# A convolution, a Fourier layer and a gated recurrence on one core: pools exchanged at the hand-over into the recurrence, first columns stored first, part of a normalisation on GpSimd

## The chip, the cores and the metric

The kernel runs on one core of one Trainium2 chip. The metric is the device time of one execution in microseconds (us), as the median of several runs. Everything is float32. Besides these times there is one profiled execution, whose trace records each instruction with its engine (PE is TensorE, DVE VectorE, ACT ScalarE, POOL GpSimd, SP SyncE) and each DMA packet.

## The reference

The input `x` has 8 samples of 32 channels of 256 x 256. Four layers follow each other, each as a residual around a group normalisation `_gn` with 16 groups:

```
x = x + fourier(_gn(x))      # rfft2, 2 x 32 x 32 modes mixed over channels, irfft2, bias
x = x + conv5x5(_gn(x))      # one 5 x 5 kernel for every channel
x = x + recurrence(_gn(x))   # a gated cell from column to column, 256 columns
x = x + mix(_gn(x))          # running maxima in four directions, 1 x 1 convolution over 5 x 32
```

The cell of the recurrence takes the column before at three heights (96 inputs) and the column itself (32 inputs):

```
r = sigmoid(r_i + r_h);  z = sigmoid(z_i + z_h);  n = tanh(n_i + r * n_h)
new = n * z + cur * (1 - z)
```

where `_i` comes from the column before and `_h` from the current, normalised column. So each column needs the one before: the recurrence is a chain of 255 steps. Its group statistics need all of the convolution's output.

## The kernel before

Four functions follow each other, each with pools of on-chip memory of its own that are opened at its start and closed at its end.

`forward_and_mix` transforms `x`, and mixes the modes with the Fourier weights in eight steps (tile `xf` holds the spectrum, `wt` the weights, `sm` the results). The mixed spectrum goes to a buffer `smd` in device memory (L287).

`inverse_and_conv` works on 16 units (sample b, half of the channels) of two times eight channels. `load_spectrum` reads `smd` back (L350, L352), `spectrum` scales and corrects it (from L358), `load` reads `x` (L379, tile `xb`, on POOL's queue), `over_rows` and `over_columns` transform back with matmuls (L401, L418) and add x into one of five large column tiles `x1` (L427). `conv` runs the 5 x 5 convolution as matmuls (L487), and L520 scales the result and adds it to `x1` in place. Squares for the statistics run on ACT (L444, L527) and DVE. `statistics` and `keep` turn them into a mean and a scale for each group (from L556, with a power on POOL at L569), held in `stb` (L575). `store` writes each `x1` to `x2d` in device memory with 12 DMAs, three for each of four row groups a: L541 the middle columns, L545 the first 30, L546 the last 30. They are on SP's queue; for the very last `x1`, half are on ACT's queue. While the last unit is under way, POOL's queue loads the first eight columns of samples 0 to 6 into the tile `first` (L659).

`recurrence` then goes through 32 blocks of eight columns. Its 8 samples are two halves of four (x is 0 and 1), which take turns: while PE works for one half, the other engines finish the other. `load` reads a block of raw columns into `xw` (L724; for block zero only sample 7 is missing in `first`, L727). The statistics are transposed into `turned` (L707), `shift` follows (L711), and `normalise` writes xn = raw * scale + shift on ACT, 128 x 256 at a time, which is one sample and half a block of columns (L733). A block is normalised while the block before it is computed, one tile in each half step; block zero is normalised in one go before the first step. In a half step, `gates` issues PE's matmuls (L753, L761), including those of the next half step on the current column; then sigmoids on ACT (L828, L830, L831), `n` on DVE (L829, L834), tanh (L835), the product `a` of 1 - z and the current column on POOL (L837), two operations on DVE (L840, L842) that give the new column `hs`, and the sum with the raw column on POOL (L843). L840 is made to wait for `a`:

```
product = nc.gpsimd.tensor_tensor(a, zm, cur, ALU.mult)
...
ins = nc.vector.tensor_tensor(m, m, z, ALU.mult)
tc.add_manual_dep(ins.ins, product.ins.name, AFTER, reason="the sum behind it then need not wait")
```

DVE also keeps a running maximum `fm` (L864) and block statistics `bst` (L875).

`maxima_and_mix` reads the stored columns and maxima and computes the last layer.

Each engine runs its instructions in the order in which the program issues them. Pools are laid one after another in memory in the order in which they are opened. A tile that lies where a tile of a closed pool lay waits for what used it, and where it lies over a pool of tiles that live for the whole stage, it waits for all uses of that pool. In the inverse stage the pools are opened as

```
one = ctx.enter_context(tc.tile_pool(name="a2c", bufs=1))   # bias, junk, x1
xp = ctx.enter_context(tc.tile_pool(name="a2x", bufs=1))    # spectra, x
wk = ctx.enter_context(tc.tile_pool(name="a2w", bufs=2))    # tt
```

so `x1` lies low and x and spectra above it; in the recurrence `one` (`turned`, `shift2`, `hs`, `bst`) lies lowest, then `xn`, `xw` and `fm` in one pool, then the small tiles of a step (`rs`, `n`, `zm`, `a`, `zs`).

Of the kernel before, what the change touches and what calls it, by code (L numbers as in the profile page):

```python
# [16 lines left out]
P = 128  # L17
# [6 lines left out]
A = 4  # L24
# [272 lines left out]
def inverse_and_conv(tc, k, d, smd, xmean, x2d, stb, first):  # L297
# [13 lines left out]

    PLACES = (1, 2, 3, 5, 6, 7, 8)
    with ExitStack() as ctx:
        one = ctx.enter_context(tc.tile_pool(name="a2c", bufs=1))
        xp = ctx.enter_context(tc.tile_pool(name="a2x", bufs=1))
        wk = ctx.enter_context(tc.tile_pool(name="a2w", bufs=2))
        sm = ctx.enter_context(tc.tile_pool(name="a2s", bufs=3))
        ps = ctx.enter_context(tc.tile_pool(name="a2p", bufs=1, space=PSUM))

# [214 lines left out]
        def store(u, ch):  # L534
            b, h = units[u]
            c0 = 2 * CH * h + CH * ch
            x1, to = x1_of(u, ch), x2d[b, :, :, c0 : c0 + CH].rearrange("w a c q -> w a (c q)")
            for a in range(A):
                r = 32 * a
                queue = nc.scalar if a % 2 and 2 * u + ch == 2 * n - 1 else nc.sync  # L540
                queue.dma_start(  # L541
                    out=to[TS + 2 : TS * (NT - 1) + 2, a].rearrange("(t w) n -> w t n", w=TS),
                    in_=x1[r + 2 : r + 30, 2:NT].rearrange("w t c q -> w t (c q)"),
                )
                queue.dma_start(out=to[0 : TS + 2, a], in_=x1[r : r + 30, 1].rearrange("w c q -> w (c q)"))  # L545
                queue.dma_start(  # L546
                    out=to[TS * (NT - 1) + 2 : W, a], in_=x1[r + 2 : r + 32, 0].rearrange("w c q -> w (c q)")
                )

        def statistics(u):  # L550
            b, h = units[u]
# [20 lines left out]
        def keep(u, st):  # L572
            b, h = units[u]
            for kind in range(2):
                nc.vector.tensor_copy(  # L575
                    by_pair(stb[:, kind, b, 2 * CH * h : 2 * CH * (h + 1)]), twice(st[:, kind], 2)
                )
# [15 lines left out]
        with tc.manual_schedule(engines=None):  # L593
# [20 lines left out]
            for u in range(n):  # L614
# [44 lines left out]
                            nc.gpsimd.dma_start(out=first[:, b], in_=columns(x2d, b, 0, 8))  # L659
                if more:  # L660
                    squares(u + 1, 1, 1, 1, NT)
            keep(n - 1, statistics(n - 1))
            store(n - 1, 1)
            tc.declare_fence(nc.tensor.drain().ins, group="conv")
# [19 lines left out]
def recurrence(tc, k, d, x2d, x3d, fwd, stb, first, loaded, mean1, mv3):  # L684
# [9 lines left out]
    BC = B // NC  # L694
    with ExitStack() as ctx:
        one = ctx.enter_context(tc.tile_pool(name="bc", bufs=1))
        blk = ctx.enter_context(tc.tile_pool(name="bb", bufs=2))
        wk = ctx.enter_context(tc.tile_pool(name="bw", bufs=2))
        ps = ctx.enter_context(tc.tile_pool(name="bp", bufs=1, space=PSUM))
# [12 lines left out]

        hs = [[one.tile([P, BC, Q + 2], F32, name=f"hs_{x}_{i}") for i in range(NH)] for x in range(NC)]
        for t in hs[0] + hs[1]:
            nc.vector.memset(t, 0.0)
        bst = one.tile([P, B, NB, 6], F32, name="bst")

        raws, norms, psums = {}, {}, {}
# [1 line left out]
        def load(bi):  # L720
            if bi:
                t = blk.tile([P, B, WB, Q], F32, name=f"xw_{bi}", tag="xw", bufs=4)
                for b in range(B):
                    nc.sync.dma_start(out=t[:, b], in_=columns(x2d, b, bi * WB, (bi + 1) * WB))  # L724
            else:
                t = first
                nc.sync.dma_start(out=t[:, B - 1], in_=columns(x2d, B - 1, 0, 8))  # L727
            raws[bi] = t
            norms[bi] = blk.tile([P, B, WB, Q], F32, name=f"xn_{bi}", tag="xn")

        def normalise(bi, b, half):
            w = slice(half * WB // 2, (half + 1) * WB // 2)
            nc.scalar.activation(  # L733
                norms[bi][:, b, w], raws[bi][:, b, w], AF.Identity, bias=shift[:, b : b + 1], scale=sc[:, 1, b : b + 1]
            )
# [464 lines left out]
```

## Time and profile before

| quantity | value |
|---|---|
| median of 3 runs | 3066.25 us (3065.99 to 3067.99) |
| profiled execution, its own time | 3069.01 us |
| its span, first to last instruction | 3067.2 us |
| mean granted TensorE clock | 0.956 |
| busy: PE, DVE, ACT, POOL | 2796.5, 2585.2, 1870.4, 858.2 us |
| last statistic of the convolution written (L575 ends) | 1025.84 us |
| first sigmoid of the recurrence (L828) | 1046.03 us |
| last mixed spectrum stored (L287 issued) | 292.74 us |
| first spectrum back in use (L358) | 317.74 us |

Times in a trace count from the first instruction. A row of the timeline gives start, duration, engine, source line, operation, tile written and tiles read, and in brackets the engine's idle time before it with the instruction or DMA that ended it. SPq and ACTq are a queue's DMA issues, whose duration is the time to issue, not to transfer.

### The profile page before, as it was taken

To read this page: it belongs to the slowest core of one execution; us is meant where nothing else is said; L and a number is where in the kernel's file an instruction comes from. 1 tells how busy PE (TensorE), PEld (TensorE's weight loads), DVE (VectorE), ACT (ScalarE), POOL (GpSimd) and SP (SyncE) were. 2 spreads that over 40 slices of the span, in tenths; PEclk is the share of its full clock that TensorE was granted. 3 is DMA by queue.
4 is the path that set the end of the run, shared out by engine and by line. 5 is a ranking of instruction groups with operands and counts; after the bars stand their busy time and mean duration, and the time that the engine had idled before them with its cause. 6 is when DMAs were issued, how large, how long until landed. Compare 5 with 4: busy or idle time off the path is not lost.

```text
span 3067.2 us, 111686 instructions
## 1 busy us (share of the span) xinstructions
PE 2796.5 (91%) x47736; PEld 1645.3 (54%) x47736; DVE 2585.2 (84%) x5178; ACT 1870.4 (61%) x4482; POOL 858.2 (28%) x1247
## 2 busy tenths in 40 slices
PE   7986799999999799999999999999999588888887
PEld 4665344444444466666666666666666233333333
DVE  5752587778888589999999999999999799999997
ACT  3432377676777578888888888888887222222222
POOL 0110011111111355555555555555555200000000
PEclk9985899999999899999999999999999799999998
DMA  9977577777775565667666676666764588888885
GB/s 385 392 283 222 154 230 225 218 224 219 231 221 165 146 148 139 142 158 167 148 142 141 154 167 151 144 142 149 167 157 115 180 327 329 328 330 329 330 327 226
DMA packets 468193, 655.69 MB, mean 214 GB/s; under 512 B 328784, under 2 KB 329696, under 8 KB 441456
## 3 DMA queue, kind: packets, MB, share of 16 engines
q1 hardware_dynamic: 407528, 487.89, 54.6%
q0 software_dynamic: 16784, 84.11, 8.4%
q10 hardware_dynamic: 43384, 76.55, 6.9%
q8 instruction: 374, 6.13, 0.8%
q14 instruction: 123, 1.01, 0.1%
HBM read 371.63 MB, written 272.63 MB: 210 GB/s over the span
## 4 chain that ended last, share of the span: by engine, by line
PE 69%; DVE 20%; DMA 5%; issue 3%; ACT 2%; SPq 0%; ACTq 0%; POOL 0%; DVEq 0%; POOLq 0%
PE r L753 14%; PE z L753 13%; PE vp L487 11%; PE ni L753 6%; PE nh L753 6%; PE up L418 4%; DVE rv L1012 4%; PE yp L131 3%; DMA spec<-smd 3%; DVE dq L1018 2%; DVE uq L1020 2%; DVE m L1026 2%; DVE m L1024 2%; DVE m L1022 2%; PE sp L158 2%
## 5 line engine op out<-in xcount | busy, mean ns | idle before, releaser
L761 PE MATMUL z<-hs,weights 64*64 64x256 f32 x4080 | 539.2, 382 | 0.0
L761 PE MATMUL ni<-hs,weights 64*64 64x256 f32 x4080 | 525.7, 375 | 0.0
L761 PE MATMUL r<-hs,weights 64*64 64x256 f32 x4080 | 525.0, 375 | 0.0
L843 POOL TENSOR_TENSOR xw<-xw,hs 128x256 f32<-128x256 f32 x496 | 340.2, 686 | 635.3 <-DVE hs L842 635.3
L1058 ACT ACTIVATE ot<-o,bres 128x512 f32<-128x512 f32 x256 | 155.1, 688 | 505.1 <-PE o L1043 489.7
L487 PE MATMUL vp<-x,c_conv 64*64 64x384 f32 (+5 forms) x4608 | 428.8, 491 | 4.9 <-DVE x L520 4.9
L520 DVE SCALAR_TENSOR_TENSOR x<-vp,r,x 128x128 f32<-128x128 f32 (+2 forms) x640 | 350.6, 563 | 87.9 <-PE vp L487 75.1
L837 POOL TENSOR_TENSOR a<-zm,xn 128x256 f32<-128x256 f32 x510 | 373.1, 732 | 7.0 <-ACT zm L830 6.7
L835 ACT ACTIVATE n<-n,bih 128x256 f32<-128x256 f32 x510 | 259.5, 509 | 186.4 <-DVE n L834 186.4
L1043 PE MATMUL o<-m,wsc 32*32 32x512 f32 x3072 | 228.8, 724 | 108.0 <-DVE m L1026 104.4
L753 PE MATMUL r<-hs,weights 64*64 64x256 f32 x2040 | 318.9, 389 | 4.4 <-DVE hs L842 3.4
L753 PE MATMUL z<-xn,weights 64*64 64x256 f32 x2040 | 305.8, 377 | 14.9 <-DMA xw<-x2d 14.9
L487 PEld LDWEIGHTS vp<-x,c_conv 64*64 64x64 f32 x4608 | 222.4, 132 | 180.0 <-issue 104.4
L753 PE MATMUL r<-xn,weights 64*64 64x256 f32 x2040 | 305.3, 376 | 2.1 <-ACT rs L828 2.1
L753 PE MATMUL nh<-xn,weights 64*64 64x256 f32 x2040 | 306.2, 377 | 0.0
L753 PE MATMUL z<-hs,weights 64*64 64x256 f32 x2040 | 305.3, 376 | 0.0
L753 PE MATMUL ni<-hs,weights 64*64 64x256 f32 x2040 | 305.1, 375 | 0.0
L733 ACT ACTIVATE xn<-xw,shift,turned 128x256 f32<-128x256 f32 x496 | 290.3, 586 | 0.0
L829 DVE SCALAR_TENSOR_TENSOR n<-nh,bhh,rs 128x256 f32<-128x256 f32 x510 | 246.2, 483 | 46.4 <-ACT rs L828 32.6
L761 PEld LDWEIGHTS ni<-hs,weights 64*64 64x64 f32 x4080 | 284.8, 133 | 0.3
L761 PEld LDWEIGHTS r<-hs,weights 64*64 64x64 f32 x4080 | 280.9, 131 | 0.2
L828 ACT ACTIVATE rs<-r,brz 128x256 f32<-128x256 f32 x510 | 241.7, 474 | 54.2 <-PE r L761 33.8
(162 smaller groups left out, 6230.3 us busy)
## 6 DMA issues: line engine op xcount, KB each, us to landing
xb<-in_xl_dram POOLq DMA_DIRECT2D x96, 768.0 KB, 7.6
xa<-in_xt_dram SPq DMA_DIRECT2D x64, 1024.0 KB
x<-x3d SPq DMA_DIRECT2D x32, 2048.0 KB
fw<-fwd SPq DMA_DIRECT2D x32, 2048.0 KB
out_dram<-ot ACTq DMA_DIRECT2D x64, 1024.0 KB
xw<-x2d SPq DMA_DIRECT2D x248, 256.0 KB
fwd<-fm SPq DMA_DIRECT2D x248, 256.0 KB
x3d<-xw SPq DMA_DIRECT2D x248, 256.0 KB
```

The costliest lines, as they stand in the source:

```text
L487: ins = nc.tensor.matmul(vps[bank][to, :, dst], lhsT=k.conv[r, P : P + 64] if kind == 2 else k.conv[r, o], rhs=pair_of(u, ch, g, lo, hi, s ...
L520: nc.vector.scalar_tensor_tensor(x, src[o], r1[rows, g : g + 1], x, ALU.mult, ALU.add, accum_out=s1[rows, 0, n, ch, g : g + 1])
L733: nc.scalar.activation(norms[bi][:, b, w], raws[bi][:, b, w], AF.Identity, bias=shift[:, b : b + 1], scale=sc[:, 1, b : b + 1])
L753: ins = nc.tensor.matmul(out[r], lhsT=weights[r, kind, gate, :], rhs=src[r], start=start, stop=stop)
L761: ins = nc.tensor.matmul(out[pairs[1 - i]], lhsT=weights[r, kind, gate, :], rhs=prev[r, :, q0 : q0 + Q], start=False, stop=stop,)
L828: rs = nc.scalar.activation(r, p["r"], AF.Sigmoid, bias=brz[:, 0:1])
L829: nc.vector.scalar_tensor_tensor(m, p["nh"], bhh[:, 2:3], r, ALU.add, ALU.mult)
L835: nc.scalar.activation(m, m, AF.Tanh, bias=bih[:, 2:3])
L837: product = nc.gpsimd.tensor_tensor(a, zm, cur, ALU.mult)
L843: nc.gpsimd.tensor_tensor(raw, raw, new, ALU.add)
L1043: nc.tensor.matmul(pts[b2][i][32 * j : 32 * j + 32].rearrange("p (w q) -> p w q", q=Q), lhsT=wsc[q, b2, t, :], rhs=src[j][q, b2], start=first,
L1058: nc.scalar.activation(ot[:, i], pts[b2][i], AF.Identity, bias=bres[:, b2, i : i + 1])
```

## The change

It has five parts. In `inverse_and_conv` the pool of `x1` is opened after those of x, spectra and `tt`, so that x and spectra lie low and `x1` above; in `recurrence`, `xn` gets a pool of its own, opened next to `one`, so that the lowest tiles and `xn` lie over spectra and x, and `xw`, `fm` and a step's small tiles over `tt` and `x1`. The stores of each `x1` write the first columns before the middle ones, and the last store writes the first columns of all four row groups, then all middle ones, then all last ones, on SP's queue alone. A sigmoid of one column is put ahead of the last statistics, with which the table is loaded there. The memsets of `hs` cover only the two border columns. The load of sample 7 into `first` is issued on POOL. And block zero's second half is normalised by GpSimd: samples 0 to 3 ahead of the first step, samples 4 to 7 in columns 1 and 2; GpSimd also normalises samples 0 to 3 of the first half of block one, in columns 4 and 5, and ACT starts with block one in column 2.

```
     with ExitStack() as ctx:
-        one = ctx.enter_context(tc.tile_pool(name="a2c", bufs=1))
         xp = ctx.enter_context(tc.tile_pool(name="a2x", bufs=1))
         wk = ctx.enter_context(tc.tile_pool(name="a2w", bufs=2))
+        one = ctx.enter_context(tc.tile_pool(name="a2c", bufs=1))
...
-            for a in range(A):
-                r = 32 * a
-                queue = nc.scalar if a % 2 and 2 * u + ch == 2 * n - 1 else nc.sync
...
+            last = 2 * u + ch == 2 * n - 1
+            parts = [(a, part) for a in range(A) for part in range(3)]
+            for a, part in sorted(parts, key=lambda x: x[1]) if last else parts:
+                r, queue = 32 * a, nc.sync
+                if part == 0:
+                    queue.dma_start(out=to[0 : TS + 2, a], in_=x1[r : r + 30, 1].rearrange("w c q -> w (c q)"))
+                elif part == 1:
...
+            nc.scalar.activation(junk[:, 0, 0:1], k.mhalf[:, 0:1], AF.Sigmoid)
             keep(n - 1, statistics(n - 1))
             store(n - 1, 1)
...
+        xnp = ctx.enter_context(tc.tile_pool(name="bn", bufs=2))
         blk = ctx.enter_context(tc.tile_pool(name="bb", bufs=2))
...
         for t in hs[0] + hs[1]:
-            nc.vector.memset(t, 0.0)
+            nc.vector.memset(t[:, :, 0 : Q + 2 : Q + 1], 0.0)
...
-                nc.sync.dma_start(out=t[:, B - 1], in_=columns(x2d, B - 1, 0, 8))
+                nc.gpsimd.dma_start(out=t[:, B - 1], in_=columns(x2d, B - 1, 0, 8))
             raws[bi] = t
-            norms[bi] = blk.tile([P, B, WB, Q], F32, name=f"xn_{bi}", tag="xn")
-
-        def normalise(bi, b, half):
+            norms[bi] = xnp.tile([P, B, WB, Q], F32, name=f"xn_{bi}", tag="xn")
+
+        def normalise(bi, b, half, other=False):
             w = slice(half * WB // 2, (half + 1) * WB // 2)
+            if other:
+                nc.gpsimd.tensor_scalar(
+                    norms[bi][:, b, w], raws[bi][:, b, w], sc[:, 1, b : b + 1], shift[:, b : b + 1], ALU.mult, ALU.add
+                )
+                return
...
-            for half in range(2):
-                for b in range(B):
-                    normalise(0, b, half)
+            for b in range(B):
+                normalise(0, b, 0)
+            for b in range(BC):
+                normalise(0, b, 1, True)
             for bi in range(NB):
                 for wi in range(WB):
                     if wi == WB // 2 and bi + 2 < NB:
                         load(bi + 2)
                     for x in range(NC):
                         step(bi * WB + wi, x)
-                        if bi + 1 < NB:
+                        if bi == 0 and 1 <= wi < 3:
+                            normalise(0, BC + NC * (wi - 1) + x, 1, True)
+                        if bi == 0 and 4 <= wi < 6:
+                            normalise(1, NC * (wi - 4) + x, 0, True)
+                        if bi + 1 < NB and (bi or wi > 1):
                             half, b = divmod(NC * wi + x, B)
                             normalise(bi + 1, b, half)
                     running(bi, wi)
```

More of the change, by code (lines that the diff above doesn't have):

```diff
@@ L537, in store @@
             x1, to = x1_of(u, ch), x2d[b, :, :, c0 : c0 + CH].rearrange("w a c q -> w a (c q)")
-            for a in range(A):
-                r = 32 * a
-                queue = nc.scalar if a % 2 and 2 * u + ch == 2 * n - 1 else nc.sync
[L541 to L548, printed above, removed]
+            last = 2 * u + ch == 2 * n - 1
[5 more added lines that the diff above has]
+                elif part == 1:
+                    queue.dma_start(
+                        out=to[TS + 2 : TS * (NT - 1) + 2, a].rearrange("(t w) n -> w t n", w=TS),
+                        in_=x1[r + 2 : r + 30, 2:NT].rearrange("w t c q -> w t (c q)"),
+                    )
+                else:
+                    queue.dma_start(
+                        out=to[TS * (NT - 1) + 2 : W, a], in_=x1[r + 2 : r + 32, 0].rearrange("w c q -> w (c q)")
+                    )
         def statistics(u):
@@ L726, in load @@
                 t = first
-                nc.sync.dma_start(out=t[:, B - 1], in_=columns(x2d, B - 1, 0, 8))
+                nc.gpsimd.dma_start(out=t[:, B - 1], in_=columns(x2d, B - 1, 0, 8))
             raws[bi] = t
-            norms[bi] = blk.tile([P, B, WB, Q], F32, name=f"xn_{bi}", tag="xn")
-        def normalise(bi, b, half):
+            norms[bi] = xnp.tile([P, B, WB, Q], F32, name=f"xn_{bi}", tag="xn")
+        def normalise(bi, b, half, other=False):
             w = slice(half * WB // 2, (half + 1) * WB // 2)
+            if other:
+                nc.gpsimd.tensor_scalar(
+                    norms[bi][:, b, w], raws[bi][:, b, w], sc[:, 1, b : b + 1], shift[:, b : b + 1], ALU.mult, ALU.add
+                )
+                return
             nc.scalar.activation(
```

## The prediction

> **What bounds the kernel now.** I read the page first: PE is busy 91% of the 3067.2 us and the chain of waits lies on PE.
>
> ```profile
> PE 69%; DVE 20%; DMA 5%; issue 3%; ACT 2%; SPq 0%; ACTq 0%; POOL 0%; DVEq 0%; POOLq 0%
> ```
>
> No matmul is removed, so what can be won lies where PE stands still. The slices and the timeline show two hand-overs. The large one is from convolution to recurrence; the timeline shows it (start, duration, engine, line; the bracket is idle time before and who ended it):
>
> ```profile
> 1021.29 0.95 ACT L527 ACTIVATE junk<-x 128x896 f32<-128x896 f32 x1 [1.81 <-DVE x L520]
> ...
> 1025.66 0.18 DVE L575 COPY stb<-st 128x16 f32<-128x16 f32 x1 [1.76 <-POOL st L569]
> ...
> 1034.23 0.98 DVE L707 STREAM_TRANSPOSE turned<-stb 128x768 f32<-128x768 f32 x1 [8.40 <-DMA x2d<-x]
> ...
> 1035.43 0.16 DVE L711 SCALAR_TENSOR_TENSOR shift<-turned 128x8 f32<-128x8 f32 x1
> ...
> 1035.76 7.98 ACT L733 ACTIVATE xn<-first,shift,turned 128x256 f32<-128x256 f32 x16 [13.43 <-DVE shift L711]
> 1037.88 1.12 PE L753 MATMUL z<-xn,weights 64*64 64x256 f32 x4 [14.88 <-DMA xw<-x2d]
> ...
> 1044.73 1.28 ACT L828 ACT_TABLE_LOAD   x1
> 1046.03 0.47 ACT L828 ACTIVATE rs<-r,brz 128x256 f32<-128x256 f32 x1
> ```
>
> The reader is to see three waits: the transpose of the statistics is ready at 1025.84 but waits 8.40 us for the last stores to land, because `turned` lies where the convolution's columns lay; then ACT normalises 16 + 2 tiles; then it loads a table. PE's last matmul for r ends near 1042.75, 3.3 us before the sigmoid that reads it.
>
> The small hand-over is from mixing to the inverse transform, the same view:
>
> ```profile
> 292.74 0.36 SPq L287 DMA_DIRECT2D smd<-sm  x1
> 296.54 0.52 SPq L350 DMA_DIRECT2D spec<-smd  x1
> 297.50 3.16 POOL L379 DMA_DIRECT2D xb<-in_xl_dram  x6 [83.64 <-issue]
> 317.74 0.69 DVE L358 TENSOR_SCALAR spec<-spec 64x1024 f32<-64x1024 f32 x1 [25.02 <-DMA spec<-smd]
> ```
>
> Here x is loaded (4.7 MB) only after the mixed spectrum is stored, and shares the DMA engines with the spectrum's load, which the chain waits for.
>
> Last, one half step of the recurrence in block zero:
>
> ```profile
> 1060.48 0.43 PE L753 MATMUL r<-hs,weights 64*64 64x256 f32 x2
> 1060.51 0.69 POOL L843 TENSOR_TENSOR first<-first,hs 128x256 f32<-128x256 f32 x1 [1.43 <-DVE hs L842]
> 1061.15 0.73 POOL L837 TENSOR_TENSOR a<-zm,xn 128x256 f32<-128x256 f32 x1
> 1061.38 0.51 ACT L835 ACTIVATE n<-n,bih 128x256 f32<-128x256 f32 x1 [0.36 <-DVE n L834]
> 1062.00 0.43 DVE L840 TENSOR_TENSOR n<-n,zs 128x256 f32<-128x256 f32 x1 [0.65 <-ACT n L835]
> ```
>
> The product `a` starts only when POOL's addition ends; it ends at 1061.88, 0.12 us before L840, which is made to wait for it. In the other half steps `a` ends 0.47 us before. POOL has almost no room here.
>
> **What the Trainium skill says.** "ScalarE: Activation LUTs", What ACT_TABLE_LOAD costs: about 1283 ns for a switch of sets; the trace agrees (1.28). "GPSIMD Engine Reference", 3.1 Elementwise: 2.6 cycles an element with two inputs, 1.03 to 1.8 with one, at 1.2 GHz. For 256 columns that is an estimate of 0.55 us with two; the trace has 0.69 and 0.73, so some 0.15 is fixed. "DMA: Bandwidth & Descriptors", Queues, rings and completion order: each DMA engine takes its queues in turn, packet by packet. The trace agrees: from 302 to 311 us it holds about 70 packets of 6 KB a microsecond from POOL's queue and about as many of 128 bytes from SP's. "SBUF — State Buffer", Who interferes with whom: a VectorE instruction with two SBUF inputs contends with a GpSimd one that reads SBUF. The trace fits: L864 takes from 0.67 to 1.16 us for one shape.
>
> **The change, part by part.**
>
> *Pools exchanged, and xn in its own.* In the inverse stage x, spectra and tt now lie lowest, the columns `x1` above. In the recurrence `turned`, `shift2`, `hs`, `bst` lie over spectra and x, `xn` over x, all long free. So the transpose needs only L575: 1025.9 to 1026.9, shift at 1027.1 (its 0.16 follows the transpose as before). That is 1035.6 - 1027.1 = 8.5 us. The eight full memsets (2.25 us of DVE) become strided ones of two columns, issued in the last unit but one; at some 0.07 each (as the smallest DVE rows) I charge 0.3 in all.
>
> *The wait that takes its place.* `rs`, `n`, `zm`, `a` and `xw` still lie over the columns, so the first sigmoid, first product and SP's block-one loads wait for all twelve last stores. Those now go on SP alone (ACT loses six issues). They are bound by transfer, not by issue: 2.1 MB took 1022 to 1033.3, 186 KB/us; the twelve before, on SP alone, took 969.8 to 982. Now the four first-column pieces can start at 1018.9, since they need only the first two tiles (L520 ends 1018.8), and 1.85 MB remains from 1022.2: 10 us, plus 0.7 for the load of `first`, plus 0.8 to land gives 1033.7.
>
> *Eighth `first` load on POOL.* It now waits for the first-column pieces only (landed near 1022.5), stands behind the power L569 (to 1025.63), takes 0.89 to issue, and 3.9 to 5 us to land: about 1030.5. Behind it on POOL are four normalisations, then the two additions; none is needed before `a` near 1035.4. ACT normalises sample seven at 1031; PE wants it about 6.1 us after shift, 1033.2.
>
> *ACT.* Eight normalisations (0.5 us apart) instead of 18 ahead of the sigmoid; the table load moves to 1022, where ACT is idle, a dummy sigmoid with it. So the sigmoid follows PE: before, r was complete 7.2 us after shift, so 1034.3; with the stores at 1033.7 plus or minus 1, I take 1034.6. Gain 1046.0 - 1034.6 = **11.4 us**, of which 8.5 is the wait and the rest the 10 activations and the table.
>
> *POOL inside the steps.* Eight normalisations are put into half steps of columns 1, 2, 4, 5, after the addition and ahead of the next `a`. Queued behind each are `a` and, through it, L840, L842 and PE's next gates. The kernel before has no such instruction on POOL. Bounds for T: 0.35 (one input at 1.03 cycles plus 0.15) and 1.0 (half as long again as the 0.69 row); I take 0.5, from 1.8 cycles. Four fall where `a` has 0.2 us of room with PE's own, four where it has 0.4: 4(T - 0.2) + 4(T - 0.4) = 8T - 2.4 = **1.6**, with port contention 1.8; at the ends 0.4 and 5.6.
>
> *Mixing to inverse.* `xb` now lies over `xf` and waits for the last mixing matmul (290.97) instead of the stores: it starts 6.4 us sooner, ahead of the last two stores, whose 128 packets per DMA engine now alternate with its 48 large ones. By work: POOL's data from 292.6, 12.1 us of DMA, 2.6 for the stores, landed at 307 to 308; spectrum issued 0.4 later (the bias load now stands before it), 5.5 us of data, landed near 316 to 318 against 317.6. Bounds: -4 (stores get through first) to +2; I take **-1.0**.
>
> Middle pieces second instead of first in the other 31 stores: the same bytes on the same queue, nothing waits for one piece; 0. PE's order is unchanged. After its pause PE's clock is low for a while in the trace (matmul pairs 0.43 us apart instead of 0.21 from 1047.3 to 1050.5, costing 0.9); I let it stay as it is.
>
> Sum: -11.4 + 1.8 - 1.0 + 0.3 = **-10.3 us**. The profiled execution has span 3067.2 and took 3069.0, 2.8 over the median 3066.25; its sum would give 3058.7, on the median 3056.0.
>
> **The rivals.** *Re-bound hand-over*: stores on SP at the pace of the contended set (12 in 14.8 us), or `first` landing 7 us after issue, set the sigmoid near 1038, and T is 1.0: -8 + 5.6 - 1.0 + 0.3, about -3 to -7, 3061. For it: the sigmoid really waits for all stores, with 0.6 us to spare. Against: no other loads run then.
>
> *More than forecast*: stores pass x quickly and T is 0.35: -11.4 + 0.4 - 4 + 0.3, 3051.5. The packet counts speak against.
>
> *GpSimd becomes the bound (slower)*: if one normalisation with per-partition scalars takes T, the gain of 12.1 is used up at T = 1.8, and from 1.8 the four ahead of the additions delay the first `a` too. It is slower by 0.2% from 2.3 us; at 2.5, 8 x 2.5 - 2.4 + 4 x 0.7 = 20.4, or +8, 3074. For it: the power takes 1.66 us for 8 columns, so POOL can be slow. Against: its plain operations keep to the estimate.
>
> *It does not do what it says*: `turned` could wait for the stores after all; the addresses in the built program exclude that, and xn's too.
>
> **How the numbers follow.** 0.2% is 6.1 us, about what a measurement of this kernel can tell from no change. Forecast 0.62; re-bound 0.22, of which 0.14 still over 0.2%; more 0.08; GpSimd 0.08, of which 0.07 over. Faster 0.84, same 0.09, slower 0.07. The range runs from more than forecast to just past re-bound: 3050.5 to 3062.5.
>
> **What would show it.** Right: the transpose near 1026 with no DMA as releaser, the table load near 1022, first sigmoid 1034 to 1036, block zero's half steps in columns 1, 2, 4, 5 longer by 0.1 to 0.6 us, the spectrum's scaling at 314 to 318. Wrong: the sigmoid released by a store after 1037; POOL's xn over 1 us; the spectrum after 320.

## The result and the profile after

The changed kernel takes 3055.6 us (median of five runs, 3052.2 to 3058.3); the kernel before, measured beside it, 3068.0. The ratio is 0.9955, with a 95% interval of 0.9942 to 0.9967: faster by some 12.4 us. The forecast was 3056.0, so the total is right, but partly by luck, for its parts are not: the trace shows one gain of 9.5 us that the prediction put at nothing, and GpSimd's instructions inside the steps cost 4.3 us where 1.8 were forecast.

First the line of the page with the shares of the chain of waits, after:

```profile
PE 65%; DVE 20%; issue 3%; DMA 2%; ACT 1%; POOL 1%; SPq 0%; DVEq 0%; ACTq 0%; POOLq 0%
```

DMA has fallen from 5% to 2%, and POOL, which had 0%, is on the chain now. Three per cent of the span would be 90 us, far more than was won: a chain can pass through the one or the other of two things that end together. Such shares tell where to look, not how much; the stages tell that.

The profiled executions, cut at four instructions that both have (first scaling of a spectrum L358; last copy of the statistics, L575 before and L579 after; first and last sigmoid of r, L828 and L839). Each time is the distance between starts in the timeline, in us:

| stage | before | after | difference | forecast |
|---|---|---|---|---|
| start to first L358 | 317.7 | 319.4 | +1.6 | -1.0 |
| inverse transform and convolution, to the last statistics | 707.9 | 698.4 | **-9.5** | 0 |
| hand-over, to the first sigmoid | 20.4 | 9.2 | -11.2 | -11.4 and +0.3 |
| recurrence, to the last sigmoid of r | 1354.0 | 1357.5 | +3.4 | +1.8 |
| the rest | 667.2 | 667.5 | +0.4 | 0 |
| span | 3067.2 | 3052.0 | -15.3 | -10.3 |

**Hand-over.** The timeline after (start, duration, engine, line; the bracket is idle time before, and who ended it):

```profile
1014.44 1.28 ACT L666 ACT_TABLE_LOAD   x1
...
1017.69 0.92 POOL L733 DMA_DIRECT2D first<-x2d  x1
1017.76 0.17 DVE L579 COPY stb<-st 128x16 f32<-128x16 f32 x1 [1.76 <-POOL st L573]
1017.97 0.98 DVE L713 STREAM_TRANSPOSE turned<-stb 128x768 f32<-128x768 f32 x1
...
1019.06 0.17 DVE L717 SCALAR_TENSOR_TENSOR shift<-turned 128x8 f32<-128x8 f32 x1
1019.26 3.55 ACT L744 ACTIVATE xn<-first,shift,turned 128x256 f32<-128x256 f32 x7 [3.32 <-DVE shift L717]
1019.42 2.16 POOL L740 TENSOR_SCALAR xn<-first,turned,shift 128x256 f32<-128x256 f32 x4 [0.80 <-issue]
...
1021.39 1.12 PE L764 MATMUL z<-xn,weights 64*64 64x256 f32 x4 [6.29 <-ACT xn L744]
...
1025.02 0.60 ACT L744 ACTIVATE xn<-first,shift,turned 128x256 f32<-128x256 f32 x1 [2.21 <-DMA first<-x2d]
...
1025.47 0.38 PE L764 MATMUL ni<-hs,weights 64*64 64x256 f32 x2
...
1025.68 0.42 PE L764 MATMUL r<-xn,weights 64*64 64x256 f32 x2
...
1025.98 4.62 SPq L730 DMA_DIRECT2D xw<-x2d  x6
1026.96 0.47 ACT L839 ACTIVATE rs<-r,brz 128x256 f32<-128x256 f32 x1 [1.34 <-PE r L772]
```

The transpose has no bracket: it follows the statistics at once. The table is loaded where ACT is idle. The new limit is PE's own work. It starts with ACT's fourth tile, at 1021.39, and PE stands idle for no more than 0.1 us from there to the end of r, which the sigmoid at 1026.96 waits for; until 1025.3 its granted clock is 0.50, and its matmul pairs are 0.43 us apart instead of 0.21. The load of sample 7 into `first`, the eighth of its loads, is issued at 1017.69, wanted by ACT at 1022.8 and landed at 1025.0. It comes just in time: ACT's eighth tile ends at 1025.62, and the matmul that reads it follows its forerunner at the usual distance, at 1025.68. The block-one loads show when the last stores were in: they are issued at 1025.98. So eighth load, stores and PE end within two microseconds of each other, and taking away one of them alone would win at most one.

**Mixing to inverse transform**, after:

```profile
293.53 3.21 POOL L379 DMA_DIRECT2D xb<-in_xl_dram  x6 [78.97 <-PE mp L269]
...
294.72 0.36 SPq L287 DMA_DIRECT2D smd<-sm  x1
...
310.20 0.52 SPq L350 DMA_DIRECT2D spec<-smd  x1
...
319.38 0.69 DVE L358 TENSOR_SCALAR spec<-spec 64x1024 f32<-64x1024 f32 x1 [24.68 <-DMA spec<-smd]
```

x is issued ahead of the last stores of the mixed spectrum, as forecast; the spectrum's load is issued late in turn, at 310.2. In this execution the mixing itself ended 2.0 us later than in the one before (last copies L284 at 292.98 and 291.00), on instructions that the change does not touch. From there to L358 it is 26.4 us against 26.7. That is no gain: in the four kernels below with the old pools this distance is 26.0 to 26.7, in the ten with the new ones 26.2 to 26.4. What x wins by its early start, the spectrum loses by its late issue.

**Block zero of the recurrence**, POOL and the DVE instruction that waits for it, after:

```profile
1037.10 0.55 POOL L740 TENSOR_SCALAR xn<-first,turned,shift 128x256 f32<-128x256 f32 x1
...
1037.62 0.72 POOL L848 TENSOR_TENSOR a<-zm,xn 128x256 f32<-128x256 f32 x1
1038.38 0.42 DVE L851 TENSOR_TENSOR n<-n,zs 128x256 f32<-128x256 f32 x1 [1.11 <-POOL a L848]
...
1040.01 1.06 POOL L740 TENSOR_SCALAR xn<-first,turned,shift 128x256 f32<-128x256 f32 x1
1040.11 0.71 DVE L875 TENSOR_TENSOR fm<-first,fm 128x512 f32<-128x512 f32 x1
```

`a` now starts when the normalisation ends, and L851 stands idle for it: 1.11 us instead of the 0.65 that it used to wait for tanh. The same normalisation takes 0.55 us in one half step and 1.06 in the next, where the maximum L875 (two SBUF inputs) runs beside it: 0.55 to 0.56 in four of the eight half steps, 1.05 to 1.06 in the other four.

**The stage that nobody expected.** The list of waits between 440 and 1000 us (engine, line, waited for: total us, times, longest), before:

```profile
DVE spec L358 <- DMA spec<-smd: 14.0, 3, 4.7
...
PEld tp L401 <- DVE yb L362: 7.6, 3, 2.6
PE tp L401 <- DVE yb L362: 4.9, 3, 1.7
```

and after:

```profile
DVE spec L358 <- DMA spec<-smd: 0.7, 1, 0.7
```

Six later spectra are loaded during the convolution. In the kernel before, three of them came late; VectorE waited 4.7 us for each, and TensorE, whose L401 reads the spectrum next, stood for it. The stage's 9.5 us are 3.2 for each. After, one is late by 0.7 us, and TensorE does not feel it.

### The profile page after: what moved, and what is told of

It is laid out like the page before. It is cut to its first block, busy times and chain, and to the rows that moved or that the text cites. A ratio compares the mean times of both kernels' runs of the same rounds, so it can differ in the third digit from the quotient of the medians.

```text
span 3052.0 us, 111712 instructions
## 1 busy us (share of the span) xinstructions
PE 2792.5 (91%) x47736; PEld 1644.4 (54%) x47736; DVE 2582.7 (85%) x5178; ACT 1863.4 (61%) x4471; POOL 867.0 (28%) x1260
## 4 chain that ended last, share of the span: by engine, by line
PE 65%; DVE 20%; issue 3%; DMA 2%; ACT 1%; POOL 1%; SPq 0%; DVEq 0%; ACTq 0%; POOLq 0%
PE r L764 14%; PE vp L487 13%; PE z L764 13%; PE ni L764 6%; PE nh L764 6%; PE up L418 5%; DVE rv L1028 4%; DVE dq L1034 2%; DVE uq L1036 2%; DVE m L1042 2%; DVE m L1040 2%; DVE m L1038 2%; PE tp L401 2%; PE o L1059 2%; PE mp L269 2%
## 5 line engine op out<-in xcount | busy, mean ns | idle before, releaser
L839 ACT ACTIVATE rs<-r,brz 128x256 f32<-128x256 f32 x510 | 241.4, 473 | 56.1 <-PE r L772 35.1
```

Of the source, the lines that this page charges most:

```text
L839: rs = nc.scalar.activation(r, p["r"], AF.Sigmoid, bias=brz[:, 0:1])
```

## The experiments

The stages of the profiled execution of each kernel, cut as above (us), with its median and ratio to the kernel before. The ratio's interval is some plus or minus 0.1%, 3 us, so smaller effects are read from the stages. The medians come from several chips, on which the kernel before took 3066.0 to 3070.7 us; between rows compare the ratios. A stage is one execution, and in the hand-over PE's stretch at half clock is not equally long in all: about 10 us in the changed kernel, about 13.5 in three of its variants (eighth load on SP, ACT normalises, spectra early on ACT behind the product), which lengthens their hand-over by 0.4 to 1.0 us.

| kernel | to L358 | inverse and convolution | hand-over | recurrence | rest | median | ratio (95%) |
|---|---|---|---|---|---|---|---|
| before | 317.7 | 707.9 | 20.4 | 1354.0 | 667.2 | 3068.0 | 1 |
| after | 319.4 | 698.4 | 9.2 | 1357.5 | 667.5 | 3055.6 | 0.9955 (0.9942 to 0.9967) |
| after, old store order | 320.1 | 709.0 | 9.1 | 1357.8 | 667.8 | 3062.1 | 0.9978 (0.9969 to 0.9987) |
| before, new store order | 322.4 | 698.4 | 20.1 | 1353.4 | 667.0 | 3062.8 | 0.9981 (0.9974 to 0.9987) |
| after, GpSimd behind the product | 320.5 | 699.5 | 9.3 | 1354.6 | 667.9 | 3052.4 | 0.9947 (0.9935 to 0.9959) |
| before, pools only | 318.8 | 708.4 | 17.9 | 1353.8 | 667.1 | 3069.7 | 1.0009 (1.0001 to 1.0017) |
| after, stores on ACT too | 320.8 | 699.5 | 9.5 | 1358.1 | 667.5 | 3058.3 | 0.9960 (0.9947 to 0.9973) |
| after, eighth load on SP | 319.7 | 701.7 | 10.3 | 1358.2 | 667.8 | 3057.9 | 0.9955 (0.9939 to 0.9972) |
| after, ACT normalises | 322.4 | 698.1 | 10.2 | 1355.4 | 667.5 | 3056.9 | 0.9957 (0.9942 to 0.9972) |
| after, table at the sigmoid | 319.7 | 699.0 | 10.5 | 1357.7 | 667.3 | 3057.0 | 0.9961 (0.9946 to 0.9977) |
| before, spectra early on ACT | 323.4 | 744.3 | 20.1 | 1353.4 | 667.8 | 3109.3 | 1.0126 (1.0109 to 1.0143) |
| after, behind the product, spectra early on ACT | 322.4 | 739.8 | 10.1 | 1356.4 | 667.4 | 3093.9 | 1.0078 (1.0062 to 1.0094) |
| before, spectra early on SP | 320.2 | 698.2 | 20.4 | 1352.4 | 665.7 | 3059.5 | 0.9982 (0.9974 to 0.9989) |
| after, behind the product, spectra early on SP | 321.1 | 699.1 | 9.2 | 1354.6 | 667.3 | 3051.8 | 0.9955 (0.9942 to 0.9969) |

The first column varies by up to 6 us among kernels, and all but 0.8 of it arises before the mixing ends; it is not explained here, and nothing below rests on it. The narrower memsets were not tried alone.

### Where the 9.5 us of the convolution come from

*After, with the old order of pieces in the first 31 stores:*

```diff
-            for a, part in sorted(parts, key=lambda x: x[1]) if last else parts:
+            old = [(a, part) for a in range(A) for part in (1, 0, 2)]
+            for a, part in sorted(parts, key=lambda x: x[1]) if last else old:
```

> Question: between the first scaling of a spectrum (L358) and the last statistics (L579) the changed kernel's profile is 9.5 us shorter; in the kernel before three later spectra are late by 4.7 us each (L358 waits for spec<-smd), in the changed one a single one by 0.7. This kernel is the changed one with the pieces of the first 31 stores in the old order (middle, first, last columns); the last store keeps the new order. Theory 'store order' (first columns first let the spectrum's packets through): the three waits of 4.7 us come back, about +9.5 us on the changed kernel, 3065. Rival 'addresses' (x, spectra or columns lying elsewhere in SBUF load faster): waits stay away, 3055.5. Rival 'chance of one execution': no difference in the medians, 3055.5, waits may show or not.

Measured: the stage is 709.0 us again, four spectra are late, the median rises by 6.5 us to 3062.1 (3065 expected). The addresses, which this kernel keeps, do not hold the gain.

*Before, with only the new order in the first 31 stores* (the first-columns piece issued ahead of the middle one):

```diff
+                last = 2 * u + ch == 2 * n - 1
+                if not last:
+                    queue.dma_start(out=to[0 : TS + 2, a], in_=x1[r : r + 30, 1].rearrange("w c q -> w (c q)"))
                 queue.dma_start(
                     out=to[TS + 2 : TS * (NT - 1) + 2, a].rearrange("(t w) n -> w t n", w=TS),
                     in_=x1[r + 2 : r + 30, 2:NT].rearrange("w t c q -> w t (c q)"),
                 )
-                queue.dma_start(out=to[0 : TS + 2, a], in_=x1[r : r + 30, 1].rearrange("w c q -> w (c q)"))
+                if last:
+                    queue.dma_start(out=to[0 : TS + 2, a], in_=x1[r : r + 30, 1].rearrange("w c q -> w (c q)"))
```

> The kernel before with one edit: the pieces of the first 31 stores in the new order (first columns, middle, last); the last store as it was. Store order: the spectrum waits at L358 after the first go from 4.7 us to under 1 us, -9.5 us on before, 3058. Addresses or chance: within 1.5 us of before, 3067.

Measured: 698.4 us, no spectrum late after the first, ratio 0.9981. The order of the small and large pieces moves the stage by 10 us in both kernels; the rival 'addresses' falls with it. The median is 5.8 us below the kernel before beside it, less than the 9.5 expected. 'Chance of one execution' falls too: the medians moved in both kernels. They give the order 6 to 7 us, less than in the profiles; how many spectra come late varies, from two to four in the profiles with the old order, from none to two in those with the new one.

What does the order change? The last third of a spectrum's load is 2048 packets of 128 bytes on ACT's queue (L352, issued at 495.91 before and 497.68 after). The DMA queues in the three microseconds from 6.5 us after that issue (packets, MB, share of the DMA engines; q10 is ACT's, q1 SP's stores, q0 the loads of x), before:

```profile
q0 software_dynamic: 40, 0.25, 58.8%
q1 hardware_dynamic: 122, 0.22, 31.6%
q10 hardware_dynamic: 14, 0.00, 0.4%
```

and after:

```profile
q10 hardware_dynamic: 1628, 0.21, 44.0%
q1 hardware_dynamic: 202, 0.35, 38.5%
q0 software_dynamic: 27, 0.17, 22.5%
```

After, ACT's queue moves 1628 packets while the next load of x is only starting; before, 14. The rest must then share the engines with x's packets of 6 KB, and the spectrum is in use 20.2 us after that issue (516.1) instead of 16.2 (513.9).

The order of the stores shifts the odds of such a pause; it does not decide it. In the kernel before itself three of the six loads are in time: after the last one's issue at 839.99, ACT's queue moves 1841 packets in the same three microseconds (846.49 to 849.49), with the old order. With the eighth load on SP and the new order, two loads are late by 3.0 and 3.5 us. What goes with lateness in the ten kernels that issue these loads on ACT at this place is how long ACT takes to issue the last piece: 3.6 to 5.2 us in the 44 loads that were in time, 5.3 to 5.6 in five that were late by 0.7 to 1.4, 6.4 to 7.5 in the eleven that were late by 3.0 to 6.0. Whether the long issue is a cause, or shows the same pause, is open. So is why ACT's packets pause more often when a 392 KB piece leads the store than when a 60 KB piece does: the large piece is issued equally long after the spectrum in both. That the engines take their queues in turn, as the prediction has it, does not by itself account for 14 packets of ACT's queue beside 40 of x's and 122 of SP's, with ACT's issue over at 502.3.

*Is the late spectrum the whole cost of the old order?* The kernel before, each later spectrum loaded four groups sooner:

```diff
-                    if u % 2 and u + 3 < n:
-                        if g == 2:
-                            load_spectrum(units[u + 3][0])
-                        elif g == 5:
-                            spectrum(units[u + 3][0])
+                    if u % 2 == 0 and u + 4 < n and g == 6:
+                        load_spectrum(units[u + 4][0])
+                    if u % 2 and u + 3 < n and g == 5:
+                        spectrum(units[u + 3][0])
```

> The kernel before with one edit: each later spectrum is loaded four groups sooner (group 6 of the even unit instead of group 2 of the odd one), its use unmoved, the stores in the old order. Theory 'the store order only decides whether the spectrum lands in time': no wait at L358 is left, inverse stage (first L358 to last L575, 708 us) at 698 as with the new order, -6 to -9 us, 3060. Rival 'the order of the stores helps the loads of x or the stores themselves': stays above 704, 3067.

Measured: 3109.3 us, 40 us slower; both theories fail. No spectrum is late any more, but the list of TensorE's waits now leads with

```profile
PE v L451 <- ACT junk L444: 30.7, 8, 5.1
```

ACT's timeline there:

```profile
491.83 0.47 ACTq L350 DMA_DIRECT2D spec<-smd  x1
492.34 0.61 ACTq L352 DMA_DIRECT2D spec<-smd  x1
...
492.99 6.15 ACTq L352 DMA_DIRECT2D spec<-smd  x1
499.24 0.31 ACT L527 ACTIVATE junk<-x 128x128 f32<-128x128 f32 x1 [6.43 <-DVE x L520]
```

The bracket names VectorE, but ACT starts again just when its third issue ends. ACT needs 7.3 us to issue one spectrum, and at the new place its squares, which come next, feed TensorE's sums. The same edit on the changed kernel with the normalisations behind the product shows it again:

> The changed kernel with GpSimd's normalisations inside the steps behind the product a, and the later spectra loaded four groups sooner. If the spectra's lateness is all that differs between executions in the inverse stage, that stage (first L358 to last L579) is 698 us in every execution and the time 3052, as with the normalisations behind the product alone (3052.4), less at most 0.7. Rival 'the earlier load takes the transfers of x': above 3054.

Measured: 3093.9 us, the stage at 739.8. The rival gave the sign, by another mechanism: x's transfers were not what waited.

So the same edit with SP issuing:

```diff
-            queue = nc.scalar if b > 1 else nc.sync
+            queue = nc.sync
```

> The kernel before with its spectra loaded at group 6 of the even unit as in the last experiment on this, but by SP instead of ACT; stores in the old order. Loaded by ACT there, no spectrum was late, but the inverse stage took 744 us, because ACT stood 5 us at each issue and PE waited for its squares. Theory 'a late spectrum is all that the old order costs': on SP nobody waits for the issue, no wait at L358 after the first, inverse stage 698 as with the new order, 3060. Rival 'the earlier load delays x' (PE waits in another place, or the stores behind it on SP come late): 702 to 715. Rival 'the old order costs 9 us elsewhere': 708, 3068.

Measured: 698.2 us, ratio 0.9982; in VectorE's list of waits up to 1010 us the only spectrum left is the first one, which both kernels wait for:

```profile
DVE spec L358 <- DMA spec<-smd: 24.7, 1, 24.7
```

The old order of stores is still in this kernel, and the stage is as short as with the new one. So the late spectrum is all that the old order cost, as far as the stage shows (698.2 against 698.4).

### GpSimd's normalisations

*After, each of the eight issued behind the product `a` of its half step, ahead of the addition:*

```diff
                 product = nc.gpsimd.tensor_tensor(a, zm, cur, ALU.mult)
+                if behind:
+                    normalise(*behind, True)
```

> The changed kernel with GpSimd's eight normalisations inside the steps issued behind the product a of the same half step instead of behind the addition to the raw tile. In the profile of the changed kernel block zero's first 13 half steps lose 4.2 us against before, at the eight places where a follows such a normalisation. Theory 'they stand ahead of a': GpSimd waits for hs there anyway (1.4 us in block zero), so the normalisation is hidden and the loss goes: -3.5 to -4.2 us on the changed kernel, 3051.5 to 3052. Rival 'port': the normalisation contends with VectorE's products of two SBUF inputs wherever it stands, and the addition behind it is late for the next a; half of the loss stays, 3053.5. Rival 'block zero is slow for another reason' (PE's clock after the pause): no change, 3055.5.

Measured: the recurrence falls by 2.9 us to 1354.6, the median from 3055.6 to 3052.4. POOL's timeline in that kernel:

```profile
1036.01 0.73 POOL L848 TENSOR_TENSOR a<-zm,xn 128x256 f32<-128x256 f32 x1
1036.73 1.25 POOL L740 TENSOR_SCALAR xn<-first,turned,shift 128x256 f32<-128x256 f32 x1
1038.33 0.68 POOL L856 TENSOR_TENSOR first<-first,hs 128x256 f32<-128x256 f32 x1 [0.35 <-DVE hs L855]
```

A normalisation takes even longer here, 1.25 us, with VectorE's operations with two SBUF inputs beside it; and it still ends before the addition's `hs` is there. The first theory holds for seven tenths (2.9 of 4.3). The stretching that the rival 'port' expects is there, but most of it lies in POOL's idle time; VectorE pays a part: its product L853 takes 0.70 us instead of 0.42 in one of these half steps.

*After, ACT doing all twelve* (the third argument of the calls, which sends them to GpSimd, left out):

```diff
-                normalise(0, b, 1, True)
+                normalise(0, b, 1)
```

> The changed kernel with ACT doing GpSimd's twelve normalisations: four more ahead of the first sigmoid, eight inside the steps of columns 1, 2, 4, 5. Hand-over: four tiles of 0.5 us behind the eighth, 2.0 less the 1.34 of idle, +0.7. Steps: GpSimd's 4.2 us go; ACT has per half step 2.63 us, three sigmoids, a tanh and one tile, some 2.4, so a second tile makes it late by about 0.3 in six half steps, +1.8. Sum -1.7 on the changed kernel, 3054. Rival 'ACT's lateness feeds back' (its tile stands ahead of the next sigmoid): +0.5 each, 8 x 0.5 = 4, no gain, 3056.

Measured: hand-over +1.0, recurrence -2.1, together -1.1 by the stages; the medians (3056.9 and 3055.6) do not show it. At most 0.2 of the +1.0 is the price of ACT's four more tiles: they end 9.4 us behind the last statistics (the changed kernel's sigmoid starts at 9.2), PE's r ends only at 10.0, and ACT stands idle for 0.8 us before the sigmoid. PE was at half clock until 9.6 us behind the last statistics here, and until 7.5 in the changed kernel, where its r ended at 9.0. So the forecast of +0.7 for the hand-over is not borne out, and the -2.1 of the steps (-2.4 forecast) is what ACT is worth. GpSimd in its place in the changed kernel is thus no better than ACT. Behind the product its recurrence is 0.8 us shorter than with ACT (1354.6 and 1355.4), too little for one execution of each to decide.

### The hand-over

*Before, with only the pools moved:*

```diff
-        one = ctx.enter_context(tc.tile_pool(name="a2c", bufs=1))
         xp = ctx.enter_context(tc.tile_pool(name="a2x", bufs=1))
         wk = ctx.enter_context(tc.tile_pool(name="a2w", bufs=2))
+        one = ctx.enter_context(tc.tile_pool(name="a2c", bufs=1))
...
+        xnp = ctx.enter_context(tc.tile_pool(name="bn", bufs=2))
         blk = ctx.enter_context(tc.tile_pool(name="bb", bufs=2))
```

> The kernel before with only the pools moved: x, spectra and tt below the columns, xn in a pool of its own; store order, queues, ACT's 18 normalisations, full memsets and table load as before. The transpose then follows L575 without the 8.4 us wait for stores (1026 in before's times). ACT's seven first tiles follow, but the eighth waits for first<-x2d, which stands on SP behind the twelve last stores in the old order (landing near 1033 to 1034), and the other nine tiles and the table load stand behind it: first sigmoid near 1041, -4.5 us at the hand-over. Spectra: theory 'store order' 0, so 3063; rival 'addresses' -9.5 more, 3053. Rival 'the 8.5 us of the transpose are won whole': -8.5, 3059.

Measured: no gain in the median (3069.7), 2.5 us in the hand-over. Its timeline:

```profile
1027.37 0.98 DVE L708 STREAM_TRANSPOSE turned<-stb 128x768 f32<-128x768 f32 x1
...
1031.31 3.55 ACT L734 ACTIVATE xn<-first,shift,turned 128x256 f32<-128x256 f32 x7 [7.48 <-DMA x2d<-x]
...
1038.20 4.53 ACT L734 ACTIVATE xn<-first,shift,turned 128x256 f32<-128x256 f32 x9 [3.34 <-DMA first<-x2d]
...
1043.73 1.28 ACT L829 ACT_TABLE_LOAD   x1
1045.03 0.47 ACT L829 ACTIVATE rs<-r,brz 128x256 f32<-128x256 f32 x1
```

The transpose no longer waits, yet two waits take its place: ACT's first tile stands behind ACT's own store issues, which end at 1030.8, and the eighth tile waits for its load, which stood on SP behind the stores. The 8.5 us of the transpose are worth 2.5 without the rest. The inverse stage is at 708.4 with two late spectra (10.9 us of VectorE's waits), so the addresses win nothing there either.

*After, with half of the last stores on ACT:*

```diff
-                r, queue = 32 * a, nc.sync
+                r, queue = 32 * a, nc.scalar if last and a % 2 else nc.sync
```

> The changed kernel with half of the last store's twelve pieces issued by ACT again (odd rows of A), in the new order. With only the pools moved, the transpose came 8 us sooner but ACT's first normalisation stood 7.5 us behind its own store issues. Theory 'ACT's queue': ACT normalises only after its last issue, which waits for the last statistics and blocks on the queue: first tile 3 to 5 us later, hand-over 12 to 14 us instead of 9.2, 3059. Rival 'transfer sets it' (PE waits for the eighth first piece, landing at 7 us behind the statistics, whatever ACT does): within 1 us of the changed kernel.

Measured: hand-over 9.5 us, +0.3: the rival's number, but not its mechanism. In that kernel's timeline ACT's last issue ends at 1022.1, and ACT's first tile starts 0.9 us after `shift` instead of 0.2. PE starts 0.75 us later for it and does not wait for the eighth load, which comes sooner here (ACT's eighth tile ends 6.6 us behind the last statistics instead of 7.9). That only 0.3 is left at the sigmoid is PE's clock: it is full again 7.4 us behind the last statistics, as in the changed kernel (7.5), so that less of PE's work falls into half clock. Freeing ACT's queue counts for little once the pieces go in the new order: with only the pools moved, ACT's last issue ended 3.7 us behind the last statistics, here 1.8.

*After, with the eighth load on SP:*

```diff
-                nc.gpsimd.dma_start(out=t[:, B - 1], in_=columns(x2d, B - 1, 0, 8))
+                nc.sync.dma_start(out=t[:, B - 1], in_=columns(x2d, B - 1, 0, 8))
```

> The changed kernel with the eighth load of first issued on SP behind the twelve last stores, as before, instead of on GpSimd. In the changed kernel it is issued 0.07 us before the last L579 and lands 7.3 us later, 2.2 us after ACT wants it. Theory 'behind the stores': SP's last issue ends 5.3 us behind the last L579, the load is issued there and lands some 3 to 4 us later, 1.5 us later than now: hand-over +1.5, 3057. Rival 'it lands with the stores anyway' (they share the DMA engines): 0. Rival 'it must wait until SP has room': +4.

Measured: hand-over 10.3, +1.1; its inverse stage, at 701.7, has two late spectra again (6.4 us of VectorE's waits). The load is issued 5.0 us behind the last L579 and lands 3.0 us later:

```profile
1026.31 0.39 SPq L733 DMA_DIRECT2D first<-x2d  x1
...
1029.30 0.60 ACT L744 ACTIVATE xn<-first,shift,turned 128x256 f32<-128x256 f32 x1 [2.91 <-DMA first<-x2d]
```

Issued early, among the stores, it takes 7.3 us; issued 5.1 us later, behind them, 3.0. So the early issue brings it in only 0.7 us sooner. Of the +1.1, that is 0.7; the other 0.4 is PE's clock, which is full again 9.5 us behind the last statistics instead of 7.5.

*After, without the dummy sigmoid:*

```diff
-            nc.scalar.activation(junk[:, 0, 0:1], k.mhalf[:, 0:1], AF.Sigmoid)
```

> The changed kernel without the dummy sigmoid (L666), so that the table is loaded at the first real sigmoid. Theory 'hidden behind PE': in the changed kernel ACT is idle 1.34 us there, waiting for r, and a load of 1.28 us needs no data: hand-over (last L579 to first sigmoid, 9.2 us) unchanged within 0.3, 3055.5. Rival 'on the path': the load waits with the sigmoid or ACT reaches it late, +1.3 us in the hand-over.

Measured: hand-over 10.5, +1.3: the rival.

```profile
1027.96 1.28 ACT L838 ACT_TABLE_LOAD   x1 [1.32 <-PE r L771]
1029.25 0.47 ACT L838 ACTIVATE rs<-r,brz 128x256 f32<-128x256 f32 x1
```

The load needs no data, but it waited with its sigmoid for r: it is hidden only where something placed ahead brings it forward.

### Both put together

The changed kernel with the normalisations behind the product and the spectra loaded early by SP:

> The changed kernel with GpSimd's normalisations inside the steps behind the product a, and its spectra loaded by SP at group 6 of the even unit. Nothing is late in the inverse stage of the kernel with the normalisations behind the product alone (699 us), so theory 'late spectrum' gives the same: 3052 within 1.5, with less spread between executions. Rival 'the earlier load delays x or the last stores': above 3055.

Measured: 3051.8 us (3050.4 to 3053.1). It ties with the version that has the normalisations alone moved (3052.4, 3051.1 to 3053.6); these two are the fastest found, some 3 to 4 us below the changed kernel by their medians, taken on other chips. Their ratios do not separate them from it; their recurrence stage does. The forecast of less spread is not borne out: 2.7 us here, 2.5 with the normalisations alone.

## Why the prediction was right, and where it was wrong

- **Hand-over, -11.4 forecast, -11.2 measured: right.** The transpose followed the statistics, the table load went to an idle stretch, the last stores were in 6.7 us after `shift` (forecast 6.6). PE released the sigmoid, as forecast; it came 7.7 us behind `shift` (forecast 7.5), because PE's r took 0.5 us longer at half clock than in the kernel before. One term was mis-sized: the eighth load took 7.3 us instead of 3.9 to 5. It cost nothing, by luck: at half clock PE came to it only as it was ready. "Of which 8.5 is the wait and the rest the 10 activations and the table" does not hold as a sum of parts: pools alone gave 2.5. The parts remove waits that cover one another.
- **Removing six issues from ACT** was named as part of this; with the new order it lets PE start 0.75 us sooner, of which 0.3 reaches the sigmoid.
- **POOL inside the steps, 1.8 forecast, 3.4 measured net: mechanism right, T mis-sized.** Across the eight affected half steps the trace loses 4.3 us, less 0.8 in an earlier one. That 0.8 is PE's clock and not GpSimd: before, the granted clock was 0.51 from 1047.4 to 1050.8, after the first sigmoid; in the changed kernel it is 1.00 from there on, and the slow stretch lies ahead of the sigmoid. The prediction let this stretch, which it put at 0.9, stay where it was. T is 0.55 us in four and 1.06 in four, past the 1 us that was to be a sign of being wrong. The prediction's own formula with these values is 4(0.55 - 0.2) + 4(1.06 - 0.4) = 4.0. It took "with port contention 1.8" as 0.2 more in all, though it had named the section "Who interferes with whom" of the Trainium skill's "SBUF — State Buffer" and the 0.67 to 1.16 us of L864; applied to the T of four half steps, the same factor of 1.7 would have given 0.87 and a cost of 3.1. The skill's "GPSIMD Engine Reference", 3.1 Elementwise, held for the undisturbed half: its best case of a tight loop, 1.8 cycles for each of 256 columns at 1.2 GHz, and the 0.15 fixed give an estimate of 0.53 us, against 0.55.
- **Mixing to inverse, -1.0 forecast, nothing measured: a term mis-sized**, inside its bounds. From the end of the mixing the profiled pair differs by 0.3 us, and the kernels with the old pools differ by 0.8 among themselves. The scaling came at 319.4, past the 314 to 318 that was to show it right; 2.0 us of that are a later end of the mixing, which the change does not touch.
- **The store order, forecast 0, measured -9.5 in the profile and 6 to 7 us by medians: the step that failed.** The text said "the same bytes on the same queue, nothing waits for one piece; 0." It asked who waits for the stores, and not whose transfer shares the DMA engines with them. What the runs showed in its place: SP's stores go beside the spectra's loads on ACT's queue, and the old order makes these late more often, at some 3 us for each late one. The profile before had the clue: 5% of the chain was DMA, and the waits held three late spectra; the prediction read only the first, 25 us long, and never asked what the other 14 us of L358's waits stood for.
- **The total** is nearer than its parts, by luck: unforeseen gain and unforeseen cost cancel in part. By the profiles the sum should have been -15.3 instead of -10.3: 9.5 of gain not seen, against 1.6 of GpSimd's cost and 2.6 in the first stage not foreseen, the rest 0.3. Against the profiled execution the forecast was 3058.7, and the one after took 3053.7. The medians differ by 12.4, since before's is 3068.0 over five runs where the forecast started from 3066.25, and three of the four executions of the changed kernel that were not profiled lasted longer than the profiled one, two of them by about 4 us.
- **Rivals.** GpSimd as the bound fell, since no normalisation took more than 1.06 us; the re-bound hand-over did happen in its cause (a load of 7 us), but not in its effect: issued with the last statistics, the load was in before PE came to it, and the rival's 3.4 us did not follow.

## What to carry to other kernels

When transfers are reordered, list what else is in flight on the DMA engines at that moment and who waits for it; "the same bytes on the same queue" says nothing about the other queues. Put work for an idle engine into the stretch where it waits anyway (here behind the product, before the addition), not ahead of the instruction that others wait for. And moving a load sooner is free only if the engine that issues it has time: the same early load made the stage 36 us longer on ACT and 10 us shorter on SP. Before a difference of a microsecond in one execution is put down to a change, compare PE's granted clock in the same stretch: here the clock alone moved the hand-over by up to 1.0 us.

## What the runs showed of the hardware

- A GpSimd normalisation with per-partition scalars of 128x256 f32 takes 0.55 us undisturbed and up to 1.06 (changed kernel) or 1.25 (behind the product) beside VectorE operations with two SBUF inputs. It can go the other way: in one half step of the version behind the product the normalisation kept its 0.56 us, and VectorE's product beside it took 0.70 instead of 0.42.
- A load of many 128-byte packets came to a near halt for 3 us (14 packets against 1628, and 1841 for a later load of the same execution). Loads late by 3 us or more were commoner with a large store first on another engine's queue than with a small one: 9 of 18 against 2 of 42.
- ACT's issue of the second of two loads with 2048 small packets each lasted 3.6 to 7.5 us (the first, 0.6 to 0.8), and ACT computed nothing in it.
- A load that takes 7.3 us when it is issued among stores takes 3.0 us behind them.
- PE's granted clock was 0.50 around its pause at the hand-over, for about 10 us in the changed kernel and about 13.5 in three of its variants; the longer stretch alone cost up to 1.0 us.
